# First dense pass of a macaron block on one core: gate columns of tiles 8 to 27 by Strassen products of 160 columns

## Chip, cores and metric

One core of one Trainium2 chip. The metric is the device time of one execution in microseconds (us). Before the change three runs took 1322.99, 1324.44 and 1324.73 us; the median is 1324.44.

## What is computed

The input x has 4 x 1024 rows of 1024 numbers in float32, taken as 32 tiles of 128 rows. Three residual steps follow each other: half of a gated dense layer, an attention inside each row, and the gated dense layer again, each on the row-normalised x. The dense layer is where the change lies:

```python
def _L0_ffn_ref(input, weight, bias, centroids, assignments):
    dots = jax.nn.softmax(x @ centroids.T / TEMPERATURE, axis=-1)
    hits = dots > THRESHOLD
    query_sel = jnp.any(hits, axis=1)
    cluster_sel = jnp.any(hits, axis=0)
    row_sel = cluster_sel[assignments]
    dense = x @ weight.T + bias
    return jnp.where(query_sel[:, None] & row_sel[None, :], dense, 0)

x = x + 0.5 * ffn(layernorm(x))
x = x + attention(layernorm(x))
x = x + 0.5 * ffn(layernorm(x))
```

There are 64 centroids, the threshold is 0.01 and the temperature 0.1. So a tile's product has 1024 dense columns and 64 gate columns, 1088 together, over a contraction of 1024 (8 blocks of 128). Which columns survive is known only when the gates of all rows are known (cluster_sel), which is why the pass over all tiles ends before the masked result can be added.

## The kernel before

Weights and centroids stand transposed side by side in SBUF (`wc`, 1088 columns). Each matmul takes a 128 x 128 block of the transposed, normalised x as its stationary operand (loaded by a weight load of its own) and streams columns of `wc`. A product goes to one PSUM bank, and VectorE (DVE) evicts it while adding bias or a partial sum.

**Columns.** `PARTS` (line 33) cuts the 1088 columns into 0 to 383, 384 to 767, and 768 to 1087. The third part (320 columns: 256 dense and 64 gate) is made for each tile directly by `ffn_part` (line 212), 8 matmuls; its 64 gate columns go to `gate` (line 326: maximum and difference on DVE), `gate_exp` (line 335: exponential on ScalarE, ACT) and `gated` (line 341: the query flag in `qsel`, and the running maximum over tiles in `best`). The other two parts, 768 columns, are made for two tiles a and a+1 at once by `winograd` (line 258): seven block products of four matmuls with 384 columns each, in place of eight. It works on sums of x (`token_sums`, line 243, on GpSimd, called POOL) and differences of weights (`weight_sums`, line 234, made once). Its steps, in order of issue, are products 1, 5, 2, 6, 7, 3 and 4; product 6 is accumulated onto the bank of product 1 after DVE has read it, and product 4 onto the bank of product 7 after DVE has read that. Each `yield` hands control back to the loop, which thereby sets the order of everything by hand: the schedule is manual, and each engine runs its instructions in the order in which the program issues them.

**Turns.** The loop of line 609 runs over t = 3 to 31; I call one run of it turn t. In turn t the program issues, in this order: loads of x of tile t+5 and of the same rows in blocks, tile t+4 (`loads`, line 579, on SP's queue); the spreading of scales of tile t+3 over partitions (`spread`, line 421, four small DMAs on SP); in odd turns the stores of two finished tiles; mean and variance of tile t+4 (`block_scales`, line 574: statistics on DVE at line 159, a root on ACT at line 162, scales on DVE at lines 168 and 170, and a small DMA from ACT's queue to DRAM at line 577); the logits of tile t (line 586, the 320 columns); in odd turns product 1 of the pair (t-3, t-2), in even turns product 7 of the pair begun in the turn before; the transposed x of tile t+2 out of its blocks (`from_blocks`, line 429: four operations on ACT, a transpose on DVE at line 438); the exponential of the gate; then products 5, 2 and 6 (odd turns), or 3 and 4 (even turns); the rest of the gate; in odd turns `token_sums`; and a piece of other work (`weights`, line 504: loads and sums of the weights of attention, one piece a turn; its pieces are Wq in turns 3 to 10, Wk and Wv in turns 11 to 18, the biases in turn 19, copies of `wc` in the next four, and the assignments in turn 29). So the eviction of any product of turn t stands in DVE's queue behind the statistics of tile t+4.

DMAs from SP and ACT report their end on a set of eight completion semaphores, taken in turn; a DMA that takes a semaphore waits until the DMA that had it before has landed.

**PSUM.** The pool `psum1` has four banks for the wide block products (tag st, line 276), and `bank` (line 152) hands out four more (tag mm), used in the turns by the logits.

After turn 31 the gates of all tiles are in `best`; it is transposed (line 367), makes the mask of columns (line 376), and the attention pass and the second dense pass follow. They are not touched.

## Time and profile before

| what | value |
|---|---|
| median of three runs | 1324.44 us |
| the profiled execution | 1325.35 us |
| its span in the profile | 1323.6 us |
| granted clock of TensorE over the span | 0.997 |
| turn 8 starts (logits of tile 8) | 104.40 us |
| turn 9 | 116.45 us |
| turn 10 | 131.62 us |
| turn 11 | 143.67 us |
| turn 12 | 158.29 us |
| turn 13 | 170.34 us |
| turn 31 | 410.40 us |

The turns' starts are the starts of their first logits matmul on TensorE (PE), in us from the span's start. In the profile a line such as L279 is the line of the kernel where an instruction was issued, PE is the matmul and PEld the weight load, and a name such as ff or st is the tile that is written: ff for a product by `ffn_part`, st for one by `winograd`, scd for a tile's scales in DRAM, xb for x in blocks. The duration of a matmul record includes its way through the array, so records overlap; what a matmul costs is the distance from its start to the next one's. In a timeline, each row has start, duration, engine, line, operation and tiles, a count, and in brackets the idle time ahead with what ended it; a small q marks an engine's sequencer, here a DMA being issued. In the table of groups the columns after the bar are busy us, mean ns of one, and idle us ahead.

### The profile page before, as it was taken

The numbers are of one execution on the slowest core, as the hardware profiler recorded it, in microseconds if no ns is written. First come the engines' busy times: TensorE is split into PE (matmuls) and PEld (weight loads), VectorE is DVE, ScalarE is ACT, GpSimd is POOL, SyncE is SP. The second block draws the span as 40 slices with busy tenths as digits, with TensorE's granted clock in tenths as the row PEclk, the third lists the DMA queues.
The fourth block names the chain that finished last, engine by engine and source line by source line (L and its number), as shares of the span: only waits on it lengthen the run. The fifth ranks groups of instructions, "written<-read, shape, count | busy, mean of one in ns | idle before, by whom it ended". The sixth has DMA issues, their size and how long they took to land.

```text
span 1323.6 us, 22208 instructions
## 1 busy us (share of the span) xinstructions
PE 1310.4 (99%) x8486; PEld 826.0 (62%) x8486; DVE 858.6 (65%) x1708; ACT 524.9 (40%) x843; POOL 575.4 (43%) x444
## 2 busy tenths in 40 slices
PE   8999999999999999999999999999999999999998
PEld 7666666666665666666666666666666655555554
DVE  4565654455535358878888888888877448555556
ACT  4344343434320445666666666666643200000000
POOL 3511123232112147576666666666532336534440
PEclk9999999999999999999999999999999999999999
DMA  8377667568634155566666666666551336765532
GB/s 295 78 146 162 141 159 145 136 150 183 146 88 190 39 170 157 158 191 197 188 196 194 199 190 200 179 185 200 157 149 27 104 136 219 249 201 174 177 115 80
DMA packets 295770, 213.42 MB, mean 161 GB/s; under 512 B 240048, under 2 KB 254640, under 8 KB 295664
## 3 DMA queue, kind: packets, MB, share of 16 engines
q1 hardware_dynamic: 277712, 164.00, 45.6%
q0 software_dynamic: 8736, 30.68, 6.3%
q10 hardware_dynamic: 9216, 17.33, 3.6%
q8 instruction: 67, 1.10, 0.4%
q14 instruction: 39, 0.32, 0.1%
HBM read 127.77 MB, written 84.18 MB: 160 GB/s over the span
## 4 chain that ended last, share of the span: by engine, by line
PE 91%; DVE 4%; DMA 2%; ACT 2%; issue 1%; ACTq 0%; DVEq 0%; SPq 0%
PE st L279 39%; PE ff L209 21%; PE qs L717 17%; PE tp L202 4%; PE pq L209 4%; PE sc L793 2%; PE po L835 2%; DMA x<-in_L_attn_x_dram 1%; DVE bn L159 1%; DMA scd<-sc 1%; DVE d L270 0%; PE tpw L487 0%; ACT xT L203 0%; DVE d L388 0%; PE pm L382 0%
## 5 line engine op out<-in xcount | busy, mean ns | idle before, releaser
L209 PE MATMUL ff<-wc,xT 128*128 128x320 f32 (+1 forms) x1088 | 307.5, 436 | 1.5 <-ACT xT L203 0.6
L209 PEld LDWEIGHTS ff<-wc,xT 128*128 128x128 f32 x1088 | 204.7, 190 | 92.4 <-issue 1.0
L252 POOL TENSOR_TENSOR ts<-xT 128x512 f32<-128x512 f32 x31 | 41.6, 1343 | 296.8 <-PE st L279 184.0
L279 PE MATMUL st<-wc,xT 128*128 128x384 f32 x496 | 170.2, 486 | 0.0
L270 DVE TENSOR_TENSOR d<-st,d 128x384 f32<-128x384 f32 x157 | 86.0, 550 | 122.3 <-PE st L279 121.1
L279 PEld LDWEIGHTS st<-wc,xT 128*128 128x128 f32 x496 | 94.0, 190 | 63.6 <-issue 0.4
L773 POOL TENSOR_TENSOR kd<-qk,tmask 128x1024 f32<-128x1024 f32 x32 | 60.6, 1893 | 164.9 <-DMA qk<-qkvd 137.5
L279 PE MATMUL st<-ws,ts 128*128 128x384 f32 x384 | 131.6, 487 | 0.3 <-DVE d L270 0.3
L279 PE MATMUL st<-wqkv,ts 128*128 128x384 f32 x360 | 121.3, 486 | 0.0
L388 DVE SCALAR_TENSOR_TENSOR d<-d,qsel,mask 128x1024 f32<-128x1024 f32 (+2 forms) x68 | 106.3, 1563 | 0.1
L717 PE MATMUL qs<-wc,ts_2q 128*128 128x384 f32 x312 | 106.2, 490 | 0.0
L399 POOL TENSOR_TENSOR x<-x,d 128x1024 f32<-128x1024 f32 x32 | 75.4, 2358 | 67.4 <-DVE d L388 55.5
L159 DVE BATCH_NORM_STATS2 bn<-x 128x6 f32<-128x512 f32 x132 | 84.3, 680 | 31.2 <-DMA x<-in_L_attn_x_dram 28.5
L279 PEld LDWEIGHTS st<-ws,ts 128*128 128x128 f32 x384 | 72.6, 190 | 50.2 <-issue 2.1
L279 PEld LDWEIGHTS st<-wqkv,ts 128*128 128x128 f32 x360 | 68.3, 190 | 48.1 <-issue 0.8
L162 ACT ACT_TABLE_LOAD x31 | 39.8, 1283 | 146.0 <-DVE mv L161 144.6
L203 ACT COPY xT<-tp 128x512 f32<-128x512 f32 x138 | 73.2, 581 | 30.4 <-PE tp L202 29.5
L279 PE MATMUL st<-wc,ts 128*128 128x384 f32 x248 | 85.1, 486 | 0.0
L270 DVE TENSOR_TENSOR d<-st,brow 128x384 f32<-128x384 f32 x93 | 51.2, 550 | 52.1 <-PE st L279 52.0
L717 PEld LDWEIGHTS qs<-wc,ts_2q 128*128 128x128 f32 x312 | 58.2, 190 | 40.5 <-issue 2.6
L202 PE MATMUL tp<-ident,xn 128*128 128x128 f32 x552 | 74.3, 278 | 4.2 <-ACT xn L177 2.2
L864 POOL TENSOR_TENSOR x<-x,ot 128x1024 f32<-128x1024 f32 x32 | 77.1, 2408 | 2.5
(121 smaller groups left out, 2060.2 us busy)
## 6 DMA issues: line engine op xcount, KB each, us to landing
x<-in_L_attn_x_dram SPq DMA_DIRECT2D x64, 512.0 KB, 4.6
d<-d SPq DMA_DIRECT2D x64, 512.0 KB, 4.8
out_dram<-x ACTq DMA_DIRECT2D x30, 512.0 KB, 4.3
xb<-in_L_attn_x_dram SPq DMA_DIRECT2D x108, 128.0 KB, 4.6
y<-x POOLq DMA_DIRECT2D x26, 512.0 KB, 3.1
xTd<-xT POOLq DMA_DIRECT2D x26, 512.0 KB, 5.1
xT<-xTd SPq DMA_DIRECT2D x26, 512.0 KB, 5.0
x<-y SPq DMA_DIRECT2D x26, 512.0 KB, 5.3
```

Of the source, the lines that this page charges most:

```text
L159: nc.vector.bn_stats(st[:, i, :], src[:, i * 512 : (i + 1) * 512])
L202: nc.tensor.transpose(tp[:, j, :], xn[:, k * P : (k + 1) * P], ident)
L203: nc.scalar.copy(t_[:, 4 * h : 4 * h + 4, :], tp)
L209: nc.tensor.matmul(p, src[:, k, :], wts[:, k, lo:hi], start=(k == 0), stop=(k == KT - 1))
L252: nc.gpsimd.tensor_tensor(s1, a21, a22, ALU.add)
L270: nc.vector.tensor_tensor(out, ps, other, ALU.add)
L279: nc.tensor.matmul(ps, src[:, k, :], wts[:, k, :], start=(k == 0 and onto is None), stop=(k == 3), skip_group_check=onto is not None,)
L388: nc.vector.scalar_tensor_tensor(d[:, sl], d[:, sl], qsel[which][:, t : t + 1], mask[:, sl], ALU.mult, ALU.mult)
L399: nc.gpsimd.tensor_tensor(xt[t], xt[t], dt_.pop(t), ALU.add)
L717: nc.tensor.matmul(ps, src[:, k, :], wts[:, k, :], start=(k == 0 and onto is None), stop=(k == 3), skip_group_check=onto is not None,)
L773: nc.gpsimd.tensor_tensor(kd, qk[:, :, D:].unsqueeze(2).to_broadcast([P, NBLK, 4, D]), tmask.unsqueeze(1).unsqueeze(3).to_broadcast([P, NB ...
L864: nc.gpsimd.tensor_tensor(xv, xv, ov, ALU.add)
```

## The change

For the twenty tiles of `GATED` (8 to 27) the logits product of turn t is left out. Instead `last_two` makes the 320 columns from 768 on for the pair (a, a+1) by the same scheme of seven block products, with two halves of 160 columns, so 28 matmuls with 160 columns in place of 16 with 320. The second half holds 96 dense columns and the 64 gate columns; the bias row is lengthened by 64 zeros for them. Each of its seven steps is issued just behind the same step of `winograd` (the two are zipped), so the pair's work falls into turns a+3 and a+4, that is, three and four turns after tile a's logits stood there before. It takes its PSUM banks from `bank` (five a pair). It uses the sums of x that `winograd` uses, and four weight differences of its own (`te`), made on POOL in turns 5 to 8; two of them lie in buffers that are used later (the mask and the attention bias), so the biases of attention move from turn 19 to turn 29, and the assignments from turn 29 to turn 28. The gates of a pair are made together: the exponentials at the end of the even turn, the rest in the next turn. Tiles 0 to 7 and 28 to 31 keep the logits product.

The diff, without the hunks that only follow the new signature of `blocks` and the one line that zeroes the bias's last 64 columns:

```diff
@@ -32,6 +32,8 @@
 HALF = 384
 PARTS = ((0, HALF), (HALF, 2 * HALF), (2 * HALF, EMB + NCL))
 KEPT = 6
+LAST = 2 * HALF, (EMB + NCL) // 2 - HALF
+GATED = range(8, 28)
 PAIRED = range(4, 30)
 WARM = 16
 ROWS = 26
@@ -117,7 +119,7 @@
 
     wc = const.tile([P, KT, EMB + NCL], F32, name="wc")
     wqkv = const.tile([P, KT, NQKV], F32, name="wqkv")
-    brow = const.tile([P, EMB], F32, name="brow")
+    brow = const.tile([P, EMB + NCL], F32, name="brow")
     bqkv = const.tile([P, NQKV], F32, name="bqkv")
 
 
@@ -227,13 +230,15 @@
             ffn_part(xT[t], i, dt_[t], f"3_{t}")
         del xT[t]
 
-    def blocks(wts):
-
-        return [wts[:, 4 * i : 4 * i + 4, h * HALF : (h + 1) * HALF] for i in (0, 1) for h in (0, 1)]
-
-    def weight_sums(wts, ts, engines):
-
-        w11, w12, w21, w22 = blocks(wts)
+    def blocks(wts, lo=0, n=HALF):
+
+        return [
+            wts[:, 4 * i : 4 * i + 4, lo + h * n : lo + (h + 1) * n] for i in (0, 1) for h in (0, 1)
+        ]
+
+    def weight_sums(ws, ts, engines):
+
+        w11, w12, w21, w22 = ws
         t1, t2, t3, t4 = ts
         sums = (t1, w12, w11), (t2, w22, t1), (t3, w22, w12), (t4, w21, t2)
         for engine, (o, p, q) in zip(engines, sums):
@@ -323,12 +328,71 @@
         del xT[a], xT[b]
         yield
 
-    def gate(ps, t, which):
+    def last_two(a, b, ss, ts, es):
+
+
+        s1, s2, s3, s4 = ss
+        t1, t2, t3, t4 = ts
+        lo, n = LAST
+        a11, a12, a22 = xT[a][:, :4], xT[a][:, 4:], xT[b][:, 4:]
+        w11, _, w21, w22 = blocks(wc, lo, n)
+        ca, cb = dt_[a][:, lo : lo + n], dt_[b][:, lo : lo + n]
+        b1, b2 = brow[:, lo : lo + n], brow[:, lo + n :]
+
+        def add(out, ps, other):
+            nc.vector.tensor_tensor(out, ps, other, ALU.add)
+
+        def prod(i, src, wts, onto=None):
+            ps = bank(f"la{i}_{a}")[:, :n] if onto is None else onto
+            for k in range(4):
+                nc.tensor.matmul(
+                    ps,
+                    src[:, k, :],
+                    wts[:, k, :],
+                    start=(k == 0 and onto is None),
+                    stop=(k == 3),
+                    skip_group_check=onto is not None,
+                )
+            return ps
+
+        def apart(t, ps):
+
+            m = EMB - lo - n
+            add(dt_[t][:, lo + n :], ps[:, :m], c[:, :m])
+            es[t] = small.tile([P, NCL], F32, tag="ge", bufs=4, name=f"ge_0_{t}")
+            add(es[t], ps[:, m:], c[:, m:])
+            gate(es[t], t, 0, es[t])
+
+        u = prod(1, a11, w11)
+        add(ca, u, b1)
+        yield
+        v = prod(5, s1, t1)
+        yield
+        p = prod(2, a12, w21)
+        add(ca, p, ca)
+        yield
+        prod(6, s2, t2, onto=u)
+        c = small.tile([P, n], F32, tag="gc", bufs=1, name=f"gc_{a}")
+        add(c, u, b2)
+        add(c, v, c)
+        add(cb, u, b1)
+        yield
+        y = prod(7, s3, t3)
+        apart(b, y)
+        yield
+        apart(a, prod(3, s4, w22))
+        yield
+        prod(4, a22, t4, onto=y)
+        add(cb, y, cb)
+        yield
+
+    def gate(ps, t, which, e=None):
 
         nm = f"{which}_{t}"
         mx = small.tile([P, 1], F32, tag="gmx", name=f"gmx_{nm}")
         nc.vector.tensor_reduce(mx, ps, AX.X, ALU.max)
-        e = small.tile([P, NCL], F32, tag="ge", bufs=4, name=f"ge_{nm}")
+        if e is None:
+            e = small.tile([P, NCL], F32, tag="ge", bufs=4, name=f"ge_{nm}")
         nc.vector.tensor_scalar(e, ps, mx, None, ALU.subtract)
         return e
 
@@ -411,6 +475,13 @@
         xb = {}
         ts = [stage.tile([P, 4, HALF], F32, tag=f"ws{i}", name=f"ws{i}") for i in range(4)]
 
+        n = LAST[1]
+        te = [const.tile([P, EMB], F32, tag="mask", name="te0"), bqkv] + [
+            stage.tile([P, 4 * n], F32, tag=f"te{i}", name=f"te{i}") for i in (2, 3)
+        ]
+        te = [i[:, : 4 * n].rearrange("p (k c) -> p k c", c=n) for i in te]
+        esums = weight_sums(blocks(wc, *LAST), te, [nc.gpsimd] * 4)
+
         def load_blocks(t):
 
             xb[t] = row(f"xb_{t}").rearrange("p (k i c) -> p k i c", k=KT, i=4)
@@ -470,7 +541,7 @@
             xt[1] = row("x1_1")
             nc.vector.memset(xt[1][:, :1], 0.0)
             nc.sync.dma_start(out=xt[1], in_=rows(xf, 1))
-            nc.sync.dma_start(out=brow, in_=bias.partition_broadcast(P))
+            nc.sync.dma_start(out=brow[:, :EMB], in_=bias.partition_broadcast(P))
             for c in (5, 0, 1, 2, 3, 4):
                 load_w(c)
             for t in range(2, 5):
@@ -531,7 +602,7 @@
                     nc.gpsimd.tensor_copy(
                         by_head(wqkv[:, k, :], i), kv[i].rearrange("p (d h) -> p d h", h=HKV)
                     )
-            elif step == 2 * KT:
+            elif step == NT - 6:
                 bn = row("bn_q").rearrange("p (c r) -> p c r", r=REP)
                 nc.sync.dma_start(
                     out=bn.rearrange("p c r -> p (c r)"),
@@ -557,19 +628,19 @@
                 nc.sync.dma_start(out=wtd[i], in_=blocks(wc)[i])
             elif step == 2 * KT + 6:
                 next(qsums)
-            elif step == NT - 6:
+            elif step == NT - 7:
                 asg = load_assigned()
                 yield
                 hot.append(one_hot(asg))
 
         pending = iter(())
-        sc, sb, ss, es = {}, {}, {}, {}
+        sc, sb, ss, es, ge = {}, {}, {}, {}, {}
         hot = []
         wtd = [dram.tile([P, 4, HALF], F32, tag=f"wtd{i}", name=f"wtd{i}") for i in range(4)]
 
         w11, w12, w21, w22 = blocks(wc)
         qts = w12, w11, w21, w22
-        qsums = weight_sums(wqkv, qts, [nc.gpsimd] * 4)
+        qsums = weight_sums(blocks(wqkv), qts, [nc.gpsimd] * 4)
 
         def block_scales(t):
             sc[t] = dram.tile([P, 2], F32, tag="scd", bufs=5, name=f"scd{t}")
@@ -599,7 +670,7 @@
                     columns(c)
                 ss[0] = token_sums(xT, 0, 1, 1)
             if t == 1:
-                for _ in weight_sums(wc, ts, [nc.gpsimd] * 4):
+                for _ in weight_sums(blocks(wc), ts, [nc.gpsimd] * 4):
                     pass
             if t + 2 < BLOCKED:
                 ahead(t + 2)
@@ -617,27 +688,40 @@
                     nc.sync.dma_start(out=d1[i], in_=dt_.pop(i))
             if t + 4 < NT:
                 block_scales(t + 4)
-            es[t] = logits(t)
+            if t not in GATED:
+                es[t] = logits(t)
             if t == 3:
                 xT[4] = transposed(xn.pop(4), "1_4")
             if t % 2 == 1:
                 a = t - 3
-                steps = winograd(a, a + 1, ss.pop(a), ts, psum1, 1, held=t == NT - 1)
+                s4 = ss.pop(a)
+                steps = winograd(a, a + 1, s4, ts, psum1, 1, held=t == NT - 1)
+                if a in GATED:
+                    for i in (a, a + 1):
+                        dt_[i] = row(f"d1_{i}")
+                    steps = zip(steps, last_two(a, a + 1, s4, te, ge))
             if t < NT - 1:
                 next(steps)
             if t > 3:
                 for i in (5, 6) if t == 4 else (t + 2,):
                     if i in sb:
                         xT[i] = from_blocks(i, sb.pop(i))
-            for i in range(4) if t == 3 else (t,):
-                es[i] = gate_exp(es[i], i, 0)
+            for i in sorted(es):
+                if i >= t - 3 and not isinstance(es[i], tuple):
+                    es[i] = gate_exp(es[i], i, 0)
             if t == NT - 1:
-                gated(es.pop(t), t, 0)
+                for i in sorted(es):
+                    gated(es.pop(i), i, 0)
                 break
             for _ in range(2 + t % 2):
                 next(steps)
-            for i in (t - 3, t) if t < 6 else (t,):
+            for i in (t - 3, t) if t < 6 else sorted(es):
                 gated(es.pop(i), i, 0)
+            if t % 2 == 0:
+                for i in sorted(ge):
+                    es[i] = gate_exp(ge.pop(i), i, 0)
+            if 5 <= t < 9:
+                next(esums)
             if t % 2 == 1:
                 ss[t - 1] = token_sums(xT, t - 1, t, 1)
             for _ in pending:
```

More of the change, by code (lines that the diff above doesn't have):

```diff
@@ L128 @@
         nc.vector.memset(b, 0.0)
+    nc.vector.memset(brow[:, EMB:], 0.0)
     ctx.enter_context(tc.manual_schedule())
@@ L970 @@
                     if k == 0:
-                        sums = weight_sums(wc, ts, [nc.vector] * 4)
+                        sums = weight_sums(blocks(wc), ts, [nc.vector] * 4)
                     for _ in range(2):
@@ L1032, in ahead_3 @@
                 tail = dt_[t][:, PARTS[2][0] :]
-                nc.gpsimd.tensor_tensor(tail, tail, brow[:, PARTS[2][0] :], ALU.add)
+                nc.gpsimd.tensor_tensor(tail, tail, brow[:, PARTS[2][0] : EMB], ALU.add)
             return token_sums(xT, a, a + 1, 2)
```

## The prediction

> **What bounds the kernel now.** I read the page first, then the matmul and weight-load groups kept apart by shape, then the timelines of PE, DVE, SP and ACT around turns 8 to 12 of the first pass (turn t is the t-th run of the loop over tiles), then DMA times to landing by stage.
>
> ```profile
> span 1323.6 us, 22208 instructions
> ...
> PE 1310.4 (99%) x8486; PEld 826.0 (62%) x8486; DVE 858.6 (65%) x1708; ACT 524.9 (40%) x843; POOL 575.4 (43%) x444
> ```
>
> PE is busy all the time, so the end moves by PE time removed plus PE waits created. The other engines matter only where PE comes to wait for them. One fp32 matmul is two records (512 matmuls of 320 columns, x1024).
>
> ```profile
> L209 PE MATMUL ff<-wc,xT 128*128 128x320 f32 x1024 | 286.3, 433 | 1.5 <-ACT xT L203 0.6 <-DVE d L270 0.5 <-DVE wc L490 0.4
> L209 PEld LDWEIGHTS ff<-wc,xT 128*128 128x128 f32 x1088 | 204.7, 190 | 92.4 <-issue 1.0 <-ACT xT L203 1.0 <-DVE d L270 0.7
> ```
>
> Turn 9 on PE: the logits product (ff), then Strassen steps 1, 5, 2 and 6, where step 6 adds onto the bank of step 1.
>
> ```profile
> 116.45 4.47 PE L209 MATMUL ff<-wc,xT 128*128 128x320 f32 x16
> 120.76 2.74 PE L279 MATMUL st<-wc,xT 128*128 128x384 f32 x8
> 123.34 2.74 PE L279 MATMUL st<-ws,ts 128*128 128x384 f32 x8
> 125.92 2.74 PE L279 MATMUL st<-wc,xT 128*128 128x384 f32 x8
> 128.96 2.82 PE L279 MATMUL st<-ws,ts 128*128 128x384 f32 x8 [0.30 <-DVE d L270]
> ```
>
> The fifth line is the one that decides: step 6 already waits for DVE (step 2 begins at 125.92 and its eight records take 2.58, so step 6 was due at 128.50: 0.47 us lost). Why DVE is late there, in SP's, ACT's and DVE's own timelines:
>
> ```profile
> 111.55 0.33 ACTq L577 DMA_DIRECT2D scd<-sc  x1
> 117.36 0.33 SPq L149 DMA_DIRECT2D x<-in_L_attn_x_dram  x1
> 123.93 1.29 DVE L159 BATCH_NORM_STATS2 bn<-x 128x6 f32<-128x512 f32 x2 [1.53 <-DMA x<-in_L_attn_x_dram]
> 127.16 0.16 DVE L168 RECIPROCAL sc<-mv 128x1 f32<-128x1 f32 x1 [1.70 <-ACT mv L162]
> 128.27 0.55 DVE L270 TENSOR_TENSOR d<-st,brow 128x384 f32<-128x384 f32 x1
> ```
>
> Scales of tile 12 leave at 111.55 and land at 117.3; x of tile 13 is issued then, because both use one completion semaphore of a set of eight taken in turn; it lands at 123.9; only then can DVE make its statistics and scales, and turn 9's evictions stand behind them in DVE's queue. Times to landing of the scales (line 577) and of x (line 149), each first around turns 8 to 12 and then later in the pass:
>
> ```profile
> L577 ACTq DMA_DIRECT2D scd<-sc x4: 326/326/338, 111.6 to 153.6; - x4
> ...
> DMA to landing us min/median/max: 5.6/5.8/6.1
> L577 ACTq DMA_DIRECT2D scd<-sc x6: 326/326/349, 179.3 to 244.3; - x6
> ...
> DMA to landing us min/median/max: 3.6/4.0/5.4
> L149 SPq DMA_DIRECT2D x<-in_L_attn_x_dram x6: 328/354/377, 89.6 to 153.0; - x6
> ...
> DMA to landing us min/median/max: 4.6/6.5/7.1
> L149 SPq DMA_DIRECT2D x<-in_L_attn_x_dram x6: 376/377/382, 179.4 to 248.4; - x6
> ...
> DMA to landing us min/median/max: 4.0/4.5/5.3
> ```
>
> A trip is slow just where the change takes cover from PE: 5.6 to 6.1 and 4.6 to 7.1 us, later 4.0 and 4.5.
>
> **The change, part by part: matmuls.** Per pair, 16 matmuls of 320 columns (32 records) become 28 of 160 (56). Start to start, 16 ff records take 120.76 - 116.45 = 4.31 us, 269 ns each; 8 records of 384 take 2.58, 322 each. The slope is 53/64 = 0.83 ns a column with 2.7 left over, so 160 columns cost 136 ns if the weight load doesn't bind. The row gives a weight load 190 ns: by it 56 x 190 = 10.64 us replace 8.62, +2.0 a pair. The Trainium skill (TensorE: Matmul & The Clock Gate, "LDWEIGHTS") counts only columns over 1.2 GHz, 107 ns for 128, under 136: then 56 x 136 = 7.61, -1.01 a pair. The trace has this nearly bare, after a transpose of 128 columns:
>
> ```profile
> 40.42 0.14 PEld L202 LDWEIGHTS tp<-ident,xn 128*128 128x128 f32 x1
> 40.53 0.95 PEld L279 LDWEIGHTS st<-wc,xT 128*128 128x128 f32 x4
> 40.63 1.13 PE L279 MATMUL st<-wc,xT 128*128 128x384 f32 x3
> ```
>
> The load of 0.19 us begins at 40.53 and its matmul at 40.63: 0.10 us later. So the record's 190 ns is mostly latency that overlaps. I take 136: ten pairs give **-10.1 us** (bounds -10.1 and +20.2).
>
> **The move.** Tiles 8 to 27 lose their logits product (4.31 us) in turn t; the narrow products run in turns 11 to 30 beside the Strassen steps. So in turns 8, 9 and 10 PE has only 7.74, 10.32 and 7.74 us of work (3, 4, 3 steps of 2.58), against 12.05, 14.6 and 12.05. PE gets there early, but the evictions that let step 4 (even turn) and step 6 (odd turn) go stand behind the statistics of tile t+4.
>
> **The new wait.** In the changed program the completion semaphores fall otherwise, because SP and ACT stand differently in the order. Before, x of every second tile waits for scales (13 for 12, 15 for 14), the scales between being waited for only by a later block load. Now x of 14 waits for scales of 13, 16 for 15, 18 for 17 and so on, and the Wq load just ahead of x of 15 for scales of 14. Every x waits for the scales before it. Behind it in SP's queue stand the blocks and scale rows; on DVE the whole turn. With no exponentials in turns 8 to 11, ACT's table load (1.28 us) before the root falls away in turns 9 to 12: statistics to scales is 3.67 (123.93 to 127.60) less 1.28 = 2.4.
>
> One trip is then scales to landing + x to landing + 2.4. By the Trainium skill (DMA: Bandwidth & Descriptors, "Anatomy of one DMA", a fit for the other path: 2.0 us plus bytes over 436 GB/s) it would be 2.0 + 3.2 + 2.4 = 7.6, and turn 10 would hardly wait. The rows are far above it: 3.9 + 4.2 + 2.4 = 10.5 (quiet), 6.1 + 7.1 + 2.4 = 15.6 (worst). I take 5.6 (the least of these turns, since the loads are now spread out) + 5.2 (x's median over the pass) + 2.4 = 13.2.
>
> Scales of 13 leave at 123.93 + 2.4 = 126.3 (x of 13 as before); of 14 at 139.55; of 15 at 153.25 (0.5 for the Wq load ahead); of 16 at 166.45; of 17 at 180.5 (x 4.2, table load again, 0.5 for Wk). PE's step can start 0.7 after (128.27 to 128.97). PE:
> turn 8 starts at 104.4; step 4 is due at 109.6, may start at 111.45 + 0.7 = 112.15: **2.5** lost. Turn 9: step 6 due at 122.5, may start at 127.0: **4.5**. Ends at 129.6. Turn 10: step 3 waits till 134.1 for the adds that free its bank (1.9), step 4 due 136.7, may at 140.2: together **5.4**. Turn 11 from 142.8 (each step now with 1.09 of narrow product): step 6 due 153.8, may 153.95: **0.15**. Turn 12: step 4 due 164.95, may 167.15: **2.2**, ends 170.8. Turn 13: due 181.8, may 181.2: nothing. From there on PE needs 25.66 a pair and two trips of the quiet size about 23, so no more waits. Sum 14.75, less the 0.47 of before: **+14.3**.
>
> **End of the pass.** The last gate's maxima reach the transpose of line 367 with 0.3 us to spare (416.98, 417.29). Now gates of 26 and 27 are folded in just ahead, 8 small DVE operations, 1.46 us, half of it while ACT works: **+0.7** (0 to 1.2).
>
> **At nothing.** Four weight differences on POOL in turns 5 to 8 (1.34 us x 640/512 = 1.7 each), under POOL's idle time; uncovered 6.7. DVE: per pair six adds of 160, two of 96 and 64 for two of 256, about +2.0 us (550 ns at 384 and 416 at 256 give 0.16 + 1.0 ns a column) with DVE 51% busy in the pass; they stand after the add that PE needs. Bias and assignment loads move to turns 28 and 29, where SP has only stores; bound 0 to 1. Five narrow banks a pair from four: each is freed a step earlier, 0 to 3, take 0. Fewer table loads help ACT, which is not on the path.
>
> **Sum.** -10.1 + 14.3 + 0.7 = **+4.9**. Check by the other road: turn 13 starts 0.5 late; seven pairs gain 7.1; turns 28 to 30 carry narrow products and logits both, +10.9; with the 0.7, +5.0. The profiled run, 1325.35 (span 1323.6 and 1.75 around it), would be 1330.2; it lies 0.9 over the median 1324.44, so **1329.3**. A measurement tells about 0.2% (2.6 us) from no change.
>
> **Rivals.**
> - Not slower: the DMA trips shrink to the quiet 10.5, as fewer transfers overlap. Turn 10 then waits 2.75, turns 11 and 12 nothing: 9.75 - 0.47 - 10.1 + 0.7 = -0.1, **1324.3**. This is its deciding point: over 10.5 a trip slower, below it a little faster, but never below -2.8, since turns 8 and 9 hang on x of 13, which nothing moved. For it: 4.0 and 4.5 later in the pass. Against: 5.6 at least for scales here. Chance 0.27.
> - The full gain, PE running ahead: **1315.0**. Against: step 6 waits already. Chance 0.04.
> - Weight loads bind at 190 ns: +20.2 with turns 8 to 10 waiting still (+11.9) and 0.7: **1357**. Against: 40.53 to 40.63. Chance 0.04.
> - Slower as forecast: chance 0.65, up to the worst trip, whose waits sum to 22: +12, 1336.5 (about 0.1 of it over 1335).
>
> Range 1321 to 1335: down to the quiet trip and somewhat below, up to nearly the worst.
>
> **What would show it.** Narrow records 136 ns apart and no more; step 6 of turn 9 near 127.0 behind a DVE add; x of 14 issued right after scales of 13 land (near 132); step 4 of turn 10 near 140; waits gone from turn 13; turns 28 to 30 of 15 to 19 us. Wrong if x of 14 leaves near 127.6, if trips are near 10, or if records stand 190 apart.

## The result and the profile after

The changed kernel takes 1326.52 us (median of 20 runs, 1324.17 to 1330.44), beside 1325.23 us (20 runs, 1322.57 to 1330.33) for the kernel before on the same chip: ratio 1.0009, 95% interval 0.9999 to 1.0019, that is -0.1 to +2.5 us, no difference that can be told. The forecast was 1329.3, +4.9 us, and most of its chance (0.65) lay on slower.

The profiled execution of the changed kernel was its longest: 1330.44 us, span 1328.7, which is +5.1 us on the profiled one of before, almost the sum that was forecast. So the parts of the sum can be read in the trace, but the medians differ by only 1.3 us. From the page, the span and engines; then, from the groups kept apart by shape, the logits product, the first of the narrow products (line 348) and the group of step 4 (line 284):

```profile
span 1328.7 us, 22771 instructions
...
PE 1304.5 (98%) x8726; PEld 842.6 (63%) x8726; DVE 875.3 (66%) x1789; ACT 495.3 (37%) x821; POOL 583.3 (44%) x448
```

```profile
L212 PE MATMUL ff<-wc,xT 128*128 128x320 f32 x704 | 197.5, 434 | 1.0 <-ACT xT L206 0.6 <-DVE d L275 0.5
...
L348 PE MATMUL la<-wc,xT 128*128 128x160 f32 x160 | 25.0, 299 | 0.0
...
L284 PE MATMUL st<-ws,xT 128*128 128x384 f32 x128 | 46.0, 504 | 6.7 <-DVE d L275 6.7
```

PE is busy 5.9 us less than before in a span 5.1 us longer: it now waits. The narrow products wait for nothing. The last group, mostly step 4, waits 6.7 us for DVE, where the same group of before waited for nothing; such waits are the new thing. In the profile of before:

```profile
L279 PE MATMUL st<-ws,xT 128*128 128x384 f32 x128 | 43.9, 486 | 0.0
```

PE's timeline after the change, in turns 8 to 10 (start, duration, then in brackets the wait):

```profile
107.66 2.74 PE L284 MATMUL st<-wc,ts 128*128 128x384 f32 x8
112.72 4.41 PE L284 MATMUL st<-ws,xT 128*128 128x384 f32 x8 [2.32 <-DVE d L275]
116.92 2.92 PE L284 MATMUL st<-wc,xT 128*128 128x384 f32 x8
119.67 2.74 PE L284 MATMUL st<-ws,ts 128*128 128x384 f32 x8
122.25 2.74 PE L284 MATMUL st<-wc,xT 128*128 128x384 f32 x8
125.07 5.40 PE L284 MATMUL st<-ws,ts 128*128 128x384 f32 x16
134.50 4.42 PE L284 MATMUL st<-wc,ts 128*128 128x384 f32 x8 [4.04 <-DVE d L275]
139.79 2.85 PE L284 MATMUL st<-ws,xT 128*128 128x384 f32 x8 [0.86 <-DVE d L275]
```

The brackets count from the modelled end of the last matmul; from start to start, less the records' own 2.58 us, the losses are 2.48, 0.24, 4.20 and 1.03 (the last is 5.29 from start to start, less 2.58, less 1.68 of half clock). Two durations stand out: 4.41 and 4.42 where the same eight records elsewhere take 2.74. Those matmuls ran at half clock. The table of stretches (columns: length, PE and weight-load busy time, granted clock, DMA share, GB/s; matmuls of line 284 only) has the clock:

```profile
105.00:113.50 8.50, 6.18 (x20) 3.37 (x19) 1.00 0.64 162
113.50:117.00 3.50, 3.50 (x8) 1.86 (x7) 0.55 0.50 171
117.00:131.00 14.00, 13.39 (x41) 7.39 (x39) 0.99 0.81 111
131.00:134.00 3.00, 0.00 (x0) 0.00 (x0) 1.00 0.93 235
134.00:137.50 3.50, 3.00 (x5) 1.81 (x6) 0.55 0.73 107
```

Twice, from 1.1 us after and from 0.2 us before PE took up work again, the clock is half for 3.41 us (113.85 to 117.26 and 134.33 to 137.74), and PE loses 1.7 us each time. Nothing in the forecast had that.

The chain behind the waits, in the timelines of SP, ACT and DVE:

```profile
112.23 0.33 ACTq L648 DMA_DIRECT2D scd<-sc  x1
117.64 0.33 SPq L152 DMA_DIRECT2D x<-in_L_attn_x_dram  x1
122.10 1.28 DVE L162 BATCH_NORM_STATS2 bn<-x 128x6 f32<-128x512 f32 x2 [3.25 <-DMA x<-in_L_attn_x_dram]
124.49 0.37 ACTq L648 DMA_DIRECT2D scd<-sc  x1
130.30 0.35 SPq L152 DMA_DIRECT2D x<-in_L_attn_x_dram  x1
132.67 1.25 DVE L509 STREAM_TRANSPOSE xT<-xb 128x1024 f32<-128x1024 f32 x1 [7.75 <-issue]
136.92 1.28 DVE L162 BATCH_NORM_STATS2 bn<-x 128x6 f32<-128x512 f32 x2
139.30 0.33 ACTq L648 DMA_DIRECT2D scd<-sc  x1
```

The scales of tile 13 leave at 124.49 and take 5.7 us to land (130.2); x of tile 14 is issued at 130.30. The scales of tile 14 leave at 139.30, so a trip is 14.8 us, and the two after it are 13.0 and 13.6. All x of tiles 13 to 25 are issued within 0.6 us after the scales of the tile before have landed. Over turns 3 to 31 (36 to 415 us of the trace) SP stood 48.4 us, in 11 waits, before a load of x until scales had landed (18.0 us in 5 waits in the kernel before), and 43.2 us before loads of blocks for the same reason.

### The profile page after: what moved, and what is told of

It reads as the page before. It is cut to its first block, busy times and chain, and to the rows that moved or that the text cites. A ratio compares the mean times of both kernels' runs of the same rounds, so it can differ in the third digit from the quotient of the medians.

```text
span 1328.7 us, 22771 instructions
## 1 busy us (share of the span) xinstructions
PE 1304.5 (98%) x8726; PEld 842.6 (63%) x8726; DVE 875.3 (66%) x1789; ACT 495.3 (37%) x821; POOL 583.3 (44%) x448
## 4 chain that ended last, share of the span: by engine, by line
PE 89%; DVE 5%; issue 2%; ACT 2%; DMA 1%; SPq 1%; ACTq 0%; DVEq 0%
PE st L284 38%; PE qs L801 18%; PE ff L212 16%; PE tp L205 4%; PE la L348 4%; PE pq L212 4%; PE sc L877 2%; PE po L919 2%; DVE d L275 1%; DVE bn L162 1%; SPq L490 1%; PE tpw L558 1%; DMA scd<-sc 0%; DVE best L414 0%; DMA x<-in_L_attn_x_dram 0%
## 5 line engine op out<-in xcount | busy, mean ns | idle before, releaser
L212 PE MATMUL ff<-wc,xT 128*128 128x320 f32 (+1 forms) x768 | 218.7, 439 | 1.0 <-ACT xT L206 0.6
L212 PEld LDWEIGHTS ff<-wc,xT 128*128 128x128 f32 x768 | 144.1, 191 | 63.8 <-issue 1.2
L165 ACT ACTIVATE mv<-mv,eps 128x1 f32<-128x1 f32 x66 | 19.4, 295 | 205.0 <-DVE mv L164 198.4
L509 DVE STREAM_TRANSPOSE xT<-xb 128x1024 f32<-128x1024 f32 x27 | 33.6, 1245 | 67.2 <-ACT xb L505 52.9
```

The source lines that it names most:

```text
L212: nc.tensor.matmul(p, src[:, k, :], wts[:, k, lo:hi], start=(k == 0), stop=(k == KT - 1))
```

## The move and the narrow products apart

**Move alone.** The kernel before, with the logits of tiles 8 to 27 issued three turns later but still as 320 columns:

```diff
-            es[t] = logits(t)
+            if t not in GATED:
+                es[t] = logits(t)
+            if t - 3 in GATED:
...
+                es[t - 3] = logits(t - 3)
```

> The kernel before with the logits products of tiles 8 to 27 left as they are (8 matmuls of 320 columns for each tile), but issued three turns later, as the change does it: the move without the narrow products. The same number of matmuls as before. Theory: the hole of 12.9 us in turns 8 to 10 costs what it does in the changed kernel up to turn 10 (2.6 + 0.3 + 5.3 us of waiting, and the half clock 3.4), less in turn 12 since wide products take 1 us longer a pair; less 0.47: +8 to +11, about 1334. Rival (the narrow products themselves, with their extra evictions, make the waits): no change, 1325.

Measured: 1342.6 us (6 runs), ratio 1.0115 (1.0086 to 1.0143), about 15 us slower, above the 8 to 11 expected. The waits stand where the changed kernel has them, and turn 9's is there too, 2.96 us against 0.3 expected; turn 12 loses 2.4 us and another 1.8 at half clock behind it, where less than the changed kernel's 1.9 was expected, and three later turns lose 3.9 together, which the expectation had at nothing:

```profile
112.16 2.85 PE L280 MATMUL st<-ws,xT 128*128 128x384 f32 x8 [2.31 <-DVE d L271]
125.54 5.40 PE L280 MATMUL st<-ws,ts 128*128 128x384 f32 x16 [2.79 <-DVE d L271]
134.57 4.51 PE L280 MATMUL st<-wc,ts 128*128 128x384 f32 x8 [3.64 <-DVE d L271]
```

The place and sign of the forecast's +14.3 hold: the deferral costs, and the narrow products pay it back.

**Scales from POOL's queue.** In this program DMAs from SP and ACT share eight completion semaphores; those from POOL have their own. So a change of queue for the scales alone uncouples x from them:

```diff
-            nc.scalar.dma_start(out=sc[t], in_=own)
+            nc.gpsimd.dma_start(out=sc[t], in_=own)
```

In the changed kernel:

> The changed kernel, with the scales of a tile sent to DRAM from POOL's queue instead of ACT's; nothing else differs. Theory A (completion semaphores: each x is issued only when the scales before it have landed, so a trip is scales to landing + x to landing + 2.4): x of tiles 14 to 17 is then issued before the scales of the tile before have landed, the waits of turns 8, 10 and 12 (about 13 us with the clock's 3.4) shrink to at most 5, and the time is 1317 to 1321, ratio to before 0.994 to 0.997. Rival B (the scales' own way to DRAM and back through the blocks sets the pace of SP's loop, whoever waits for them): x is earlier but the transposes of blocks on DVE are late, waits of the same size stay: 1325 to 1330. Rival C (POOL's queue sends the scales later than ACT's, behind its sums): slower than the changed kernel, over 1330.

Measured: 1319.48 us (9 runs), ratio 0.9946 (0.9925 to 0.9967): 7 us quicker than before, as Theory A had it. SP no longer waits for scales before any load of x or of blocks (48.4 and 43.2 us in the changed kernel's trace, none in this one). x of tile 15 is issued at 118.32, while the scales of tile 13 are still under way (sent at 117.71, 7.5 us to landing) and those of tile 14 not yet made; of the waits two remain (POOL, SP, PE):

```profile
117.71 0.56 POOL L648 DMA_DIRECT2D scd<-sc  x1 [5.22 <-DVE sc L173]
118.32 1.09 SPq L152 DMA_DIRECT2D x<-in_L_attn_x_dram  x1
...
110.57 2.85 PE L284 MATMUL st<-ws,xT 128*128 128x384 f32 x8 [2.31 <-DVE d L275]
129.31 2.85 PE L284 MATMUL st<-ws,xT 128*128 128x384 f32 x8 [0.41 <-DVE d L275]
```

Rival B and Rival C are out. The profiled execution was the shortest of the nine (1315.24 us) and shows no half clock, not even at the start of the pass, where its first block product begins at 39.27 us against 41.41 in the changed kernel's; those 2.1 us are not the queue's doing, as the first scales are sent only at 41.2.

The same edit in the kernel before, as a control:

> The kernel before, with the scales sent to DRAM from POOL's queue instead of ACT's; nothing else differs. Control for the same edit in the changed kernel, which brought it from ratio 1.0009 to 0.9946. Theory A (the semaphores cost only where PE has no logits to cover the trip): before loses no more than 0.5 us to it, so ratio 0.999 to 1.000. Rival B (the edit is worth the same 8 us in either kernel, so that it says nothing on the change): ratio 0.993 to 0.995.

Measured: 1323.45 us (22 runs), ratio 0.9971 (0.9962 to 0.9981). Better than Theory A allowed, by some 3 us; the profile shows the 0.47 us of turn 9 gone, and no cause in this pass for the rest: the pass ends (transpose of `best`) at 417.13 us against 417.29, and 2.0 of the 2.2 us between the two spans lie behind it, 1.4 of them a half-clock stretch at 957.5 that only the profiled execution of before has. The remainder is open. The gain is about half of Rival B's 8 us, so the edit does say something on the change, but not with its whole effect.

And in the move alone:

> The kernel before, with the logits product of tiles 8 to 27 issued three turns later in its wide form, and the scales sent from POOL's queue; with ACT's queue this move alone gave ratio 1.0115. Theory A (most of the move's cost is x waiting for the landing of scales): what is left is as in the changed kernel with POOL's queue, 3 us of waits and up to 1.7 at half clock: 1328 to 1331 where before has 1326, ratio 1.002 to 1.004. Rival B (the cost of the move is the missing cover itself, whatever queue): ratio 1.009 to 1.012.

Measured: 1328.92 us (22 runs), ratio 1.0017 (1.0005 to 1.0028): Theory A. The waits of turns 9 and 12 are gone, 2.48 and 0.57 us stay in turns 8 and 10, and 1.5 us of half clock follow the first. Side by side, as ratios to before:

| | scales from ACT | scales from POOL |
|---|---|---|
| kernel before | 1 | 0.9971 |
| move alone, 320 columns | 1.0115 | 1.0017 |
| changed kernel, 160 columns | 1.0009 | 0.9946 |

The move costs 1.15% (15 us) by ACT's queue and 0.46% (6.1 us) by POOL's: 9 us of it (uncertain by about 4) are SP's loads waiting for scales. The narrow products give 1.06% (14 us) and 0.71% (9.4 us); by the intervals of the two ratios each is uncertain by about 0.3% (4 us and 3 us). The second, where few waits are left to mix in, agrees with the forecast's 10.1. Read along the right-hand column, the whole change is worth 0.25% (3.3 us, uncertain by about 3): nearly half of what the changed kernel gains by POOL's queue, the kernel before gains by it too.

## The order on DVE

**Statistics behind the evictions.** If evictions are late only because they stand behind the statistics, moving these to the end of the turn should free them:

```diff
-            if t + 4 < NT:
-                block_scales(t + 4)
             if t not in GATED:
                 es[t] = logits(t)
...
+            if t + 4 < NT:
+                block_scales(t + 4)
             if t % 2 == 1:
                 ss[t - 1] = token_sums(xT, t - 1, t, 1)
```

> The changed kernel, with the statistics of tile t+4 moved from the front of turn t to its end, behind the turn's evictions in DVE's queue; nothing else. Theory (the gain is eaten by PE waiting in turns 8 to 12 for evictions that stand behind statistics, which stand behind the landing of x): the waits of turns 8, 9, 10 and 12, the wait at the end of the pass excepted, go, and with them the half clock after them; the narrow products' 10.1 us remain: about 1316, 9 to 10 us under before. Rival A (narrow products cost nearly what they save, waits are only where it shows): 1325 to 1327. Rival B (the statistics are needed earlier and the stall moves to the scales' landing or to the block loads): between, with waits of PE at other places of the same turns.

> The kernel before with that same move of the statistics and nothing else. Theory: before has only 0.47 us of such a wait, so -0.5 to 0 us: 1324.7 to 1325.2. Rival (the move is a gain by itself, whatever the columns): as far under before as the changed kernel with the move is under the changed kernel, 9 us.

Measured: in the changed kernel 1332.41 us (22 runs), ratio 1.0037 (1.0023 to 1.0051), a clear miss; in the kernel before 1327.34 us (14 runs), ratio 0.9990 (0.9975 to 1.0004), within what was expected by the median, though its profiled execution (1329.5 us) has new waits of 2.33 and 1.09 us where the 0.47 went. In the first, statistics at the end of a turn stand just ahead of the first eviction of the next turn, and they in turn stand behind the transposes of blocks, and these behind ACT, which waits for rows of scales (scb) that SP sent late, because SP itself stood at x. Step 4 of turn 8 now loses 3.9 us, more than before the edit, that of turn 10 2.7, and the clock halves behind both (PE; then ACT, DVE, PE):

```profile
114.30 4.34 PE L284 MATMUL st<-ws,xT 128*128 128x384 f32 x8 [3.75 <-DVE d L275]
...
128.30 2.08 ACT L505 ACTIVATE xb<-xb,scb 128x256 f32<-128x256 f32 x4 [7.24 <-DMA scb<-scd]
130.41 1.25 DVE L509 STREAM_TRANSPOSE xT<-xb 128x1024 f32<-128x1024 f32 x1 [7.31 <-ACT xb L505]
137.53 4.54 PE L284 MATMUL st<-ws,xT 128*128 128x384 f32 x8 [2.47 <-DVE d L275]
```

So the statistics weren't got out of the way, and they weren't the only thing that holds up an eviction: an operation on DVE that waits for SP's queue does it too. With both edits, POOL's queue and statistics at the end:

> The changed kernel with both edits: scales sent from POOL's queue, and statistics and scales moved to the end of the turn, behind the evictions. Alone the first gave 0.9946 and the second 1.0037. Theory A (with the queues uncoupled, the 2.5 and 0.6 us that are left in turns 8 and 10 are statistics, root and table load standing on DVE ahead of an eviction): these go, waits before the end of pass fall from 3.1 to under 0.7, 1316 to 1318 where the first edit alone has 1319.5, ratio 0.992 to 0.994. Rival B (scales that leave later delay the blocks again, as in the second edit alone): the waits move to the transposes, 1320 to 1326, ratio 0.995 to 0.999.

Measured: 1322.38 us (22 runs), ratio 0.9966 (0.9955 to 0.9977). The time is Rival B's, not better than POOL's queue alone, but its reason isn't: at the end of turn 7 the statistics stand just ahead of the eviction of product 7 of turn 8, and the same 2.48 us stay; at the end of turn 11 they cost 2.0 us more in step 4 of turn 12, and the clock halves behind both waits (1.8 us each). DVE and PE in turn 8:

```profile
107.16 1.28 DVE L162 BATCH_NORM_STATS2 bn<-x 128x6 f32<-128x512 f32 x2
...
110.72 1.21 DVE L586 TENSOR_REDUCE wqkv<-qn 128x256 f32<-128x1024 f32 x1
111.84 0.55 DVE L275 TENSOR_TENSOR d<-st,d 128x384 f32<-128x384 f32 x1
...
112.44 4.54 PE L284 MATMUL st<-ws,xT 128*128 128x384 f32 x8 [2.32 <-DVE d L275]
```

**Statistics behind the first product.** What step 4 needs is only the eviction of product 7. So, with POOL's queue, the statistics go right behind that:

```diff
             if t < NT - 1:
                 next(steps)
+            if t + 4 < NT:
+                block_scales(t + 4)
```

(and are taken out ahead of the logits, as above).

> The changed kernel with scales sent from POOL's queue, and statistics, root and scales of a tile placed behind the first block product of the turn (product 1 or 7) and its eviction, instead of ahead of it; at the end of the turn, as tried before, they stood ahead of the next turn's first eviction and the same 2.5 us stayed. Theory A (step 4 of turn 8 waits only because the eviction of product 7 stands behind 3.5 us of statistics on DVE): step 4 of turns 8 and 10 waits under 0.3 us, no half clock follows there, and with nothing new 3 to 5 us are gained on the changed kernel with POOL's queue alone (1319.5): 1315 to 1318, ratio 0.991 to 0.994. Rival B (DVE's work in a turn of 7.7 us is too much whatever its order, so another eviction comes late): a wait of 1 to 3 us moves to step 3 of turn 10, 1318 to 1323, ratio 0.994 to 0.997.

Measured: 1318.94 us (6 runs), ratio 0.9951 (0.9933 to 0.9969). Theory A by the trace, but not by the gain: from turn 6 to turn 30 PE waits nowhere, in turns 8 to 10 its rows follow each other at 2.58 us,

```profile
109.36 2.74 PE L284 MATMUL st<-wc,ts 128*128 128x384 f32 x8
111.94 2.74 PE L284 MATMUL st<-ws,xT 128*128 128x384 f32 x8
114.52 2.74 PE L284 MATMUL st<-wc,xT 128*128 128x384 f32 x8
...
65.41 1.85 PE L212 MATMUL ff<-wc,xT 128*128 128x320 f32 x6 [1.93 <-DVE xT L509]
```

and in exchange one wait of 2.09 us is new in turn 5, at 65.41, where a logits product waits for a transpose. Its time is that of POOL's queue alone (0.9946) within the intervals, so the further 3 to 5 us were not gained: 3.05 us of waits went, 2.09 came. Both beat the kernel before by about half a per cent, of which 0.29% is what the queue gives to the kernel before as well.

## Lead, load, place and clock

**Loads a turn earlier.** In the changed kernel, from turn 3:

```diff
-            if t + 5 < NT:
-                load_x(t + 5, rows(xf, t + 5), 1)
-            if BLOCKED <= t + 4 < NT:
-                load_blocks(t + 4)
+            for i in range(t + 5 + (t > 3), t + 6 + (t >= 3)):
+                if i < NT:
+                    load_x(i, rows(xf, i), 1)
+                if BLOCKED <= i - 1 < NT:
+                    load_blocks(i - 1)
```

> The changed kernel, with the loads of x and of its blocks issued one turn earlier from turn 3 on (x of tile t+6 and blocks of t+5 in turn t); nothing else differs. Theory A (x is late in turns 8 to 12 because it is issued late): the statistics of these turns find x landed, the waits of turns 8, 9, 10 and 12 (9.9 us and 3.4 at half clock) fall to under 4 together: 1315 to 1319, ratio to before 0.992 to 0.996. Rival B (the way of the scales through DRAM and the spread is what is late, as when the statistics were moved behind the evictions): x is there but the blocks' transposes wait on DVE, and the loss stays: 1325 to 1332.

Measured: 1333.23 us (10 runs), ratio 1.0061 (1.0040 to 1.0082): Rival B. x is there when DVE wants it, but it is still issued only when scales land (x of 15 at 127.26, scales of 13 landed at 127.18), and SP's rows of scales come after it, so ACT and the transposes wait instead:

```profile
128.68 2.08 ACT L505 ACTIVATE xb<-xb,scb 128x256 f32<-128x256 f32 x4 [7.95 <-DMA scb<-scd]
130.79 1.25 DVE L509 STREAM_TRANSPOSE xT<-xb 128x1024 f32<-128x1024 f32 x1 [9.15 <-ACT xb L505]
```

A longer lead doesn't help a queue that is itself stopped.

**Small weights in the gap.** The pieces of Wk and Wv (turns 11 to 18) and of Wq (turns 3 to 10) change places:

```diff
-            if step < KT:
+            if KT <= step < 2 * KT:
...
-            elif step < 2 * KT:
+            elif step < KT:
```

> The changed kernel, with the pieces of weights loaded beside the tiles in swapped order: Wk and Wv in turns 3 to 10, Wq in turns 11 to 18, so that the large loads of Wq don't lie in turns 8 to 10, where PE has lost its logits. Theory A (slow trips, 13 to 15 us in place of 10.5, because the queues are loaded): x and scales land 1 to 2 us sooner each in turns 8 to 10, waits of turns 9 and 10 shrink by 2 to 5, but turns 12 to 18 get the load; 1321 to 1325 against 1326.5 for the changed kernel. Rival B (the time to landing doesn't depend on Wq's loads): no change against the changed kernel, 1325 to 1328.

Measured: 1328.62 us (22 runs), ratio 1.0021 (1.0009 to 1.0032). In turns 8 to 10 the scales land in 2.9 to 4.3 us and x in 3.5 to 4.3, well under the 5.6 and 5.2 of the forecast, and the losses there are 1.35, 0.18, 2.90 and 1.51 in place of 2.48, 0.24, 4.20 and 1.03: Theory A by the landings, a miss by the waits and the time. From turn 14 on ten further waits of 0.3 to 1.3 us appear, 6.9 us in all. So moving the loads shortens the trips of turns 8 to 10 and moves the waits; that the load as such sets the length of a trip is not shown (last section).

**Gated from tile 16.** `GATED = range(16, 28)`, six pairs.

> The changed kernel with the narrow products for tiles 16 to 27 only: six pairs in place of ten (saving 6 x 1.01 = 6.1 us in place of 10.1), and the turns without logits are 16 to 18, where a trip is quicker (scales 4 and x 4.5 us). Theory A (the loss is the gap of cover, and its size is by the trip's length there): trip 10.9 us against PE's 7.7 + 10.3 + 7.7 in turns 16 to 18; lost 3 to 6 in place of 13.3; with the end of pass 0.5: 1322 to 1325 where before is 1324.4, ratio 0.998 to 1.0005. Rival B (the loss comes from the start of the pass, not from the gap): nothing lost at 16 to 18: 1318 to 1319, ratio 0.9955. Rival C (the gap costs the same 13 anywhere): 1332, ratio 1.005.

Measured: 1332.1 us (15 runs), ratio 1.0041 (1.0025 to 1.0057): Rival C's number, a miss for Theory A. At the new gap, turns 16 to 18, only 5.0 us are lost (1.36, 0.31, 0.20 and 3.17), near what Theory A said; but 2.84 us are lost in turn 10, where no logits are missing, and 4 us later in the pass. In turn 10 the eviction stands behind statistics, and these behind a transpose that came late (134.02, after 6.9 us of waiting for ACT). Why that is so in turns without a gap is not settled; the edit also changes which DMAs follow each other on the semaphores.

**Fillers.** To keep PE's clock up, 20 and 35 transposes that nothing reads before step 4 of turns 8 and 10:

```diff
+                if left == 1 and t in (8, 10):
+                    for i in range(20 if t == 8 else 35):
+                        nc.tensor.transpose(bank(f"fill{t}_{i}")[:, :P], ident, ident)
```

> The changed kernel with transposes of the identity that nobody reads on PE just ahead of product 4: 20 in turn 8 (2.2 us) and 35 in turn 10 (3.8 us), both shorter than the waits there (2.5 and 4.2). Theory of the half clock: PE's idle time of 2.5 to 4.2 us is followed by records of 640 ns in place of 322; with PE kept at work, the waits stay and the half clock goes: 1.5 to 3.4 us under the changed kernel, 1323 to 1325. Rival (the long records are the matmul's own wait for operands, or the fillers only add): as the changed kernel, or 1 us slower.

Measured: 1338.01 us (6 runs), ratio 1.0072 (1.0044 to 1.0100), a miss. The clock held in turn 8 (113.09 below takes 2.85), but then turns 9 and 10 wait where there are no fillers, the clock halves behind those waits, and the 35 fillers run as work of their own, 4.3 us of it:

```profile
113.09 2.85 PE L284 MATMUL st<-ws,xT 128*128 128x384 f32 x8
...
126.39 7.09 PE L284 MATMUL st<-ws,ts 128*128 128x384 f32 x16 [2.71 <-DVE d L275]
136.28 4.08 PE L284 MATMUL st<-wc,ts 128*128 128x384 f32 x8 [2.80 <-DVE d L275]
140.15 4.45 PE L719 MATMUL fill<-ident 128*128 128x128 f32 x35
```

What was saved in turn 8 came back as a longer wait in turn 9 (2.9 us in place of 0.24), as it would if the DMA trip, not PE, sets when turn 9 goes on. A wait of 3.5 us in turn 24 is new as well.

## Why the prediction was right, and where it wasn't

**Narrow products: right.** Eight records of 160 columns take 1.09 us from start to start (145.05 to 146.14), 136 ns each, and no narrow record stands back for its weight load. With POOL's queue and statistics behind the first product, free of waits, a pair of turns takes 25.66 us (191.25 to 216.91), as forecast; before, 26.67 (143.67 to 170.34). The rival of 190 ns is out.

```profile
191.25 2.74 PE L284 MATMUL st<-wc,xT 128*128 128x384 f32 x8
193.83 1.25 PE L348 MATMUL la<-wc,xT 128*128 128x160 f32 x8
194.91 2.74 PE L284 MATMUL st<-ws,ts 128*128 128x384 f32 x8
...
216.91 2.74 PE L284 MATMUL st<-wc,xT 128*128 128x384 f32 x8
```

**The coupling: right.** x of 14 was to leave at 132 behind the scales of 13; it left at 130.30, about 0.1 us after they landed. The trip was to be 13.2; it is 14.8, 13.0 and 13.6. POOL's queue removes it, and with it 9 of the move's 15 us.

**The waits: right in kind, their sum near by luck** (profiled execution, us):

| step | forecast | measured |
|---|---|---|
| turn 8, step 4 | 2.5 | 2.48 |
| turn 9, step 6 | 4.5 | 0.24 |
| turn 10, steps 3 and 4 | 5.4 | 5.23 |
| turn 11 | 0.15 | 0 |
| turn 12, step 4 | 2.2 | 1.91 |
| later, turns 18 and 24 | 0 | 2.13 |
| half clock behind turns 8 and 10 | not in the sum | 3.4 |
| end of the pass | 0.7 | 0.53 |
| sum | 15.45 | 15.9 |

The waits alone are 12.5 us; that the sum comes out near 15.45 is luck, since 3.4 us of half clock, which the forecast didn't have, fill in for turn 9. Turn 9 is the step that failed: "step 6 due at 122.5, may start at 127.0". It might start at 125.07, as x of 13 came 1.8 us earlier than before (bn at 122.10, forecast 123.93), and it was due only at 124.83, because turn 8's half clock had already held PE up: PE came later than forecast, and DVE earlier. The move alone, whose turn 8 ran at full clock, shows the two apart: there step 6 was due at 122.6, as forecast, and lost 2.96 us. In turn 10 the forecast 134.1 and 140.2 for steps 3 and 4 became 134.50 and 139.79, but step 3's eviction stood there behind the block transposes that SP's queue held up (132.67), not only behind statistics. The quiet trips that the forecast took for everything behind turn 13 did not last either: from 280 us on the scales take 4.9 to 7.0 us to land (3.2 to 7.3 in the kernel before, whose rows were read only up to 244), and turn 24 loses 1.7 us.

The balance of the two profiled executions is then -10.1 + 15.9 - 0.5 (turn 9's wait of before) = +5.3. Two things outside the change belong to it: a longer half-clock stretch at the start of the pass, by which turn 8 begins 0.7 us later (105.08 against 104.41), and a half-clock stretch of before at 957.5 in the second pass (granted clock 0.57 over 4 us, 1.4 us lost), which the changed kernel's execution does not have. With both the sum is +4.6 against +5.1 seen; 0.5 us are not accounted for.

**Slower as forecast: wrong by the medians.** +1.3 us (-0.1 to +2.5) isn't +4.9. The likeliest case, 0.65, did not come; the "not slower" case did, but its reason, a trip of 10.5, is not what the profiled execution shows. So the time lies in a range that reached from below no change to nearly the worst trip, and the sign that was thought likeliest is not confirmed. What the other nineteen executions spared, no trace shows. A candidate is the clock: a wait of 2.48 us in step 4 of turn 8 stands in five profiled executions (changed kernel, move alone with either queue, POOL's queue, both edits), and in three of them the clock halved behind it, in two it did not, so that up to 3.4 us of the profiled +5.1 may come and go (the last section shows on what it hangs). The granted clock on record for all twenty runs bears this out in part: the five at 0.995 or less, the profiled one among them, take 1329.2 us on average, the fifteen at 0.996 or more 1326.0, but among these fifteen the time doesn't follow the clock. The kernel before moves with its clock too (148 runs beside the experiments: 1324.3 us at 1.000, 1331.0 at 0.995 or less). In which turns the clock halved in runs without a profile is not known, so how much of the gap it explains stays open.

The end of the pass: the transpose of `best` waits 0.53 us where it waited for nothing, as forecast to 0.2; turns 28 to 30 take 15.31, 18.97 and 15.31 us.

```profile
420.72 2.74 PE L284 MATMUL st<-wc,xT 128*128 128x384 f32 x8
423.83 0.27 PE L431 MATMUL bT<-ident,best 128*64 128x128 f32 x1 [0.37 <-DVE best L414]
```

## What to carry to other kernels

Work that is saved on the engine that bounds the kernel is also cover for what other queues do meanwhile: before deferring a product, look for the loop of DMAs and small operations that it hid, and price that loop's trip against the shortened turn. Two DMAs that have nothing to do with each other can wait for each other, here through a shared completion semaphore; where a tile's load leaves within half a microsecond after another DMA has landed, turn by turn, try another queue first, since a longer lead did not help (1.0061) and another queue did (0.9946). And put the eviction that the next product needs ahead of any operation that waits for a load. Try such a change of queue on the kernel before as well, or its own gain is credited to the change.

## What the hardware showed that was not expected

The clock halves behind waits shorter than its window. The Trainium skill (TensorE: Matmul & The Clock Gate, "HAM oscillation") warns of idle gaps over about 3.4 us, and "What's actually happening" there has a free-running window of 3413 ns. The half-clock stretches here last 3.41 us, and those of turns 8 and 10 begin 20.48 us apart (113.85 and 134.33), six times that, as a free-running window would have it. But they follow waits of 2.3 us already (turn 8), below that limit; of five equal waits of 2.48 us three were followed by one; and the wait of 3.5 us in turn 24 of the kernel with fillers was followed by none (granted clock 1.00 from 351 to 359 us). What decides is how a wait lies to the windows, which each trace fixes, since all its stretches begin whole multiples of 3.413 us apart. In the first pass of the fourteen traces, behind turn 4, all 15 stretches follow a window in which PE stood for 2.0 us or more. One window with 2.2 us was followed by none, and so were all nine waits of 1.9 to 3.5 us that the windows cut into pieces of under 1.9 us, the two unpunished waits of 2.48 us among them. By these figures, as an estimate, a wait of 2.48 us leaves 2 us in one window in somewhat over half of its possible places. A forecast that adds waits of over 2 us on PE should add 0 to 1.7 us for each.

Times to landing vary by more than a factor of two for the same transfer: 1 KB of scales took 4.0 to 5.7 us in turns 8 to 12 of the changed kernel, and 2.9 to 4.3 in turns 8 to 10 where only the small weights were loaded beside it. The load of weights can't be the whole reason: from 322 to 357 us of the changed kernel, when none are loaded or copied, they took 4.9 to 5.5 us.
